# Attention with a depthwise convolution: the first image ends like the middle ones, the first q and k piece follows the projection, and constant products run at the start

## The chip, the core and the metric

The kernel runs on one core of a Trainium2 chip. A core has TensorE (PE in the profile, its weight loads PEld), VectorE (DVE), ScalarE (ACT), GpSimd (POOL) and SyncE (SP). Each engine works through its own instructions in order; data transfers are issued by SP, ACT or POOL instructions and run beside the engines. The metric is the time of one execution in microseconds (us) on the device; less is better.

## The reference

The input x holds 16 images of 384 channels and 32 x 32 points. Two layers follow each other, each with a residual:

```python
x = x + attention(_gn(x), w_qkv, w_proj, b_proj)     # 8 heads of 48 channels, softmax over 1024 points
x = x + depthwise_conv7x7(_gn(x), w_sym)             # w_sym: mean of the four rotations of weight
```

`_gn` normalises 32 groups of 12 channels to mean 0 and variance 1 over all points of a group. All is float32.

## The kernel before

**Tiling.** Channels lie on the 128 partitions, three tiles (k or o = 0, 1, 2) to an image. The heads are taken in pairs: unit u = 4b + p is pair p of image b. A unit has two halves of 512 query points, and each half eight steps, one for every 128 key points. So an image has 64 steps, in eight groups of eight (r = 0, 8, ..., 56).

**A step.** `s_step` (L466) makes the scores of both heads in one PSUM buffer, and ScalarE takes the exponential out of it (L480). `av_step` (L482) multiplies with the values. The values carry a column of ones, so the row sums of the softmax come out of the same products. After eight steps `take` (L499) copies a half out of PSUM. The tag "s" has three PSUM buffers, shared by scores, q and k, values and projections, in turn.

**The order.** The program order is written out by hand: the scheduler of the framework is off (`manual_schedule`). The main loop (L1155) writes, for each group: eight `s_step`; in the group r = 0 of an image also its value products (`v_step`, L442, 15.7 us on PE); a slot for other work; eight `av_step`; another slot. A planner counts two clocks in us, `clock` for PE and `vclock` for VectorE, with fixed costs (L808). `after(wait, cost, f)` puts off a piece of VectorE's work, `catch_up` (L872) writes what is due and fills up with convolution taps, `applies` with `act_slot` (L967) holds ScalarE's pieces with a due time and a cost, and `other` (L1111) starts a projection if one is due, or else the next piece of q and k of the next image (`chunks`; one piece is two `qk_step`, L414, 12 products and two ScalarE copies, L428). The last piece, "rest", is six copies between partitions on SP (L437).

**A middle image's end.** `finish` (L1022) sends the row sums out through DRAM (SP, L506 and L507), `invert` takes the reciprocal on 16 columns and spreads it back (L513 to L519), `divide` multiplies (L524), and the fourth unit's rows are copied to the other three (six SP transfers, L529), so that the projection needs three packed weights `w_packed`. This takes place while the next image's first scores and values are made. Then `project` (L913) writes three `proj_step` (L534: 6 products, an ACT output with the row sum, a POOL transfer that adds x, L556); behind the second it writes the normalisation of the image after next on ScalarE (`x_apply`, L338, three tiles). Then come the statistics of the result x1: `x1_means` on VectorE (L943), `x1_squares` on ScalarE (L270), a trip through DRAM on POOL (`gather_x1`, L276 and L278), `aggregate` (L282), `groups_x1` on ScalarE (L288 to L290), a second trip on POOL (`spread`, L259 and L263), and `x1_chains` (L974): ScalarE normalises three tiles (L338), and VectorE starts the 49 taps of each (L607).

**The ends of images 0 and 15** (`FAST`, L139) are different: the sums are spread by a product with a mask (`divide_at_once`, L568), the reciprocal is taken on 512 columns (L570), and the projection is split into parts with four weights, one for each unit (`proj_part`, L579; weights `w4` in `wp` and `w3`). For image 0, `fast_finish` and `fast_end` lie between its last value products and image 1's first ones. `fast_end` makes the statistics with one-column products on PE (`groups_on_pe`, L307) and normalises on POOL, ACT and DVE. At the start, image 0's own x is normalised with `groups_on_pe` too.

**Once only.** In image 0, VectorE takes the statistics of the images 2 to 15 as they stream in. At the end of group r = 0 of image 1, `conv_prepare` (L632) is written: on POOL a memset, two transfers to DRAM, 16 transfers back (L648, which wait for the first), eight transfers of zeros (L658, L659) and four small operations on `eye` (L663, L665). They prepare the part of the last two images' convolution that PE does. After it SP loads `wp` anew with `w_packed` (L1206).

Of the kernel before, what the change touches and what calls it, by code (L numbers as in the profile page):

```python
# [16 lines left out]
P = 128  # L17
# [27 lines left out]
def kernel(  # L45
# [64 lines left out]
    def run(general):  # L110
        tag = "g" if general else "f"
        with ExitStack() as stack:
# [20 lines left out]
            def psum(name):  # L133
                return ps_s.tile([P, 2, HALF], F32, tag="s", name=name)
# [1 line left out]
            xns, x1s, qks, os_, accs, es, xn1s = {}, {}, {}, {}, {}, {}, {}  # L136
            xds, shs, pss, mats, psums = {}, {}, {}, {}, {}
            PE_K = [NK - 1, NK - 2]
            FAST = (0, B - 1)  # L139

            PE_TILES = [(b, k) for b in (B - 2, B - 1) for k in PE_K]
            SHARED = None if general else (B - 2, PE_K[1])
# [27 lines left out]
            w4 = w_proj_4.rearrange("(t p) c -> p t c", p=P)  # L170
            w_packed = w_proj_t.rearrange("(k p) c -> p k c", p=P)
            late, pps = {}, {}
            if general:
                nc.sync.dma_start(wp, w_packed)
            else:
                nc.sync.dma_start(wp, w4[:, 0:NK])
                late["w3"] = npool.tile([P, N], F32, tag="xn1", name="w3_0")[:, 0:C]
                nc.sync.dma_start(late["w3"], w4[:, NK])
            bp = wpool.tile([P, NK], F32, name="bp")
            with nc.allow_non_contiguous_dma(reason="one small vector"):  # L180
                nc.sync.dma_start(bp, b_proj.rearrange("(k p) -> p k", p=P))
# [379 lines left out]

            def divide_at_once(u, h):
                half = os_[u][:, h * HALF : (h + 1) * HALF]
                ps = ps_o.tile([P, HALF], F32, tag="acc", name=f"ps_sum_{u}_{h}")
# [249 lines left out]
            def now():  # L817
                return vclock if catching else max(clock, vclock)

            def after(wait, cost, f):  # L820

                nonlocal count
                count += 1
                heapq.heappush(later, (now() + wait, count, cost, f))
# [88 lines left out]
            def project(b):  # L913
                nonlocal clock
                for o in range(NK):
                    proj_step(b, o)
                    clock += US_PROJ
                    if b in ON_VECTOR:
                        after(8.0, 1.3, lambda o=o: x1_part(b, o))

                    if o == 1 and pending:
                        pending.pop()()
                if b not in ON_VECTOR:
                    after(1.6, 0.2, lambda: x1_means(b))

            def x1_part(b, k):

# [12 lines left out]
            def x1_means(b):  # L940
                st = x1_stats[b] = Stats(f"x1_{b}")
                st.bs = x1_bs[:, b % 2]
                nc.vector.scalar_tensor_tensor(  # L943
                    st.bs[:, :, 1::3],
                    psums.pop(b).unsqueeze(2).to_broadcast([P, NK, 2]),
                    -1.0 / N,
                    x_mean[:, b, :].unsqueeze(2).to_broadcast([P, NK, 2]),
                    ALU.mult,
                    ALU.add,
                )  # L950
                applies.append((now() + 4.5, 4.2, lambda: x1_squares(b, st)))

            def x1_squares(b, st):
                for k in range(NK):
                    st.square(x1s[b, k], k)
                st.gather_x1()
                after(11.0, 0.6, lambda: x1_aggregate(b, st))
# [16 lines left out]
            def x1_chains(b, st):  # L974
                on_pe = [t for t in PE_TILES if t[0] == b]
                for k in range(NK - 1, -1, -1):
                    conv_begin(st, b, k, (nc.gpsimd, None, nc.vector)[k] if b in (0, B - 1) else None)
                    if (b, k) in on_pe:
                        conv_store(b, k)
                        pe_conv.extend(  # L980
                            (b, k, h, part)
                            for h in range((b, k) == SHARED, 2)
                            for part in range(2)
                        )
                after(
                    2.0 if b == B - 1 else 6.0,
                    0.0,
                    lambda: chains.extend(
                        (b, k) for k in range(NK) if (b, k) not in on_pe or (b, k) == SHARED
                    ),  # L990
                )
# [29 lines left out]

            def finish(u):  # L1022
                sums_out(u)
                if u % NP < NP - 1 or u // NP not in FAST:
                    waiting.add(u)
                    after(6.0 if u % NP == NP - 1 else 9.0, 0.3, lambda: finish2(u))

# [11 lines left out]
            def queue(b):  # L1039
                chunks.extend(("qk", b, i) for i in range(6))  # L1040
                chunks.append(("rest", b, 0))

            st = Stats("x_0")
            for k in range(NK):
                st.channels(xns[0][:, k, :], k)
# [2 lines left out]
            for k in range(NK):  # L1048
                engine = (nc.vector, None, nc.vector)[k]
                st.apply(xns[0][:, k, :], xns[0][:, k, :], k, engine)  # L1050
            conv_weights()
            ready[0] = 0.0
            queue(0)
            every = [(b, k) for b in range(2, B) for k in range(NK)]
# [100 lines left out]
            for b, n0, size in [  # L1155
                (b, b * PER_B + sum(SIZES[:g]), SIZES[g]) for b in range(B) for g in range(len(SIZES))
            ]:
                r = n0 - b * PER_B
                if n0 == NS - PER_B:
                    last_image = clock  # L1160
                if r == 0:
                    while chunks:
                        issue(chunks.popleft())
                    if b + 1 < B:
                        queue(b + 1)
                for n in range(n0, n0 + size):
                    s_step(n)
                clock += (size * US_STEP + US_TURN) / 2
                if r == 0 and b - 1 == FAST[0]:
                    fast_end(b - 1)  # L1170
                if r == 0:
                    for i in range(NT // 2):
                        issue(("v", b, i))
                ending = b in FAST and r + size == PER_B
                if ending:
                    catch_up(clock)
                    divide_at_once(NP * b + NP - 1, 0)
                    vclock += 4.2
                    for o in range(NK):
                        proj_part(b, o, (0, 1))  # L1180
                    clock += 2 * US_PROJ
                else:
                    if r and pending and b - 1 in FAST:
                        applies.append((clock, 3.7, pending.pop()))
                    catch_up(clock)
                    act_slot(4.5)
                    other(r + size, False)
                for n in range(n0, n0 + size):
                    av_step(n)
                    u, h, i = n // (2 * NT), n // NT % 2, n % NT  # L1190
                    if i == NT - 1:
                        take(u, h)
                clock += (size * US_STEP + US_TURN) / 2
                if n0 // (2 * NT) < (n0 + size) // (2 * NT):
                    finish((n0 + size) // (2 * NT) - 1)
                if ending:
                    catch_up(clock)
                    assert not invs and not waiting
                    fast_finish(b)
                else:  # L1200
                    other(r + size, True)
                if b == B - 4 and r == 32:
                    after(0.0, 2.0, check_early)
                if b == 1 and r == 0:
                    conv_prepare()
                    nc.sync.dma_start(wp, w_packed)  # L1206
                if b == B - 1:

                    if once("mat_0", r >= 16):
                        mat = flat2(xpool.tile([P, NK, N], F32, tag="x", name="mat_0"))  # L1210
                        conv_matrices(0, mat)
                        late["w3"] = mat[:, 2 * SH * KS * CH :][:, 0:C]
                    if once("w", r >= 32 and b - 1 in x1_stats):
                        nc.sync.dma_start(wp, w4[:, 0:NK])
                        nc.sync.dma_start(late["w3"], w4[:, NK])
                    if once("mat_1", r >= 24):
                        conv_matrices(1, flat2(qkpool.tile([P, 2, N], F32, tag="qk", name="mat_1")))
                    if once("ones", r >= 32):
                        t = opool.tile([P, N], F32, tag="o", name="masks_1")
                        nc.sync.dma_start(t, masks.rearrange("p b c -> p (b c)"))  # L1220
                        late["masks"] = t.rearrange("p (b c) -> p b c", c=P)
                if b in FAST:
                    if r >= 32 and (b, 0) not in x1s and all(c[0] > b - 2 for c in active):
                        for k in range(NK):
                            x1s[b, k] = rpool.tile([P, N], F32, tag="x1", name=f"x1_{b}_{k}")
                            nc.gpsimd.dma_start(
                                x1s[b, k], x[b, k * P : (k + 1) * P].rearrange("p h w -> p (h w)")
                            )
                if b == B - 1 and r in (32, 40, 48):
                    loads(1)  # L1230
# [63 lines left out]
```

## Time and profile before

| | |
|---|---|
| median of 3 runs | 2950.46 us (2949.72 to 2952.27) |
| the profiled execution's own time | 2951.93 us |
| its span, from first to last instruction | 2950.1 us |
| mean granted TensorE clock | 0.997 |
| period of a middle image on PE (its projection at 426.12, the next at 601.4) | 175.3 us |
| ACT exponentials L480 | 952.4 us in 1024, 1054 ns each |
| DVE taps L607 | 2352.8 us in 2181, 1154 ns each |
| q and k products L421 | 509.1 us, 1152 records |

A line of the page or of an answer gives a source line, an engine, an operation, the tiles it writes and reads with their shapes, a count, and a busy time. In brackets stands how long the engine sat idle before it, and what ended that. A timeline line begins with start and length in us from the span's start; instructions of the same kind are merged. Lines for waits have the waiting line, what it waited for, the sum in us, how often, and the longest. A row of windows has the stretch, its length, the busy time of PE, PEld, DVE, ACT and POOL with instruction counts, the granted clock (1.00 is full), and the share and rate of the transfers.

The start in short: x lands by 7.9 us, VectorE's statistics are done at 9.6, two rounds of averages with one-column products run on PE from 9.67 and 13.47 (3.15 us each), and the first q product starts at 19.00.

### The profile page before, as it was taken

To read this page: it belongs to the slowest core of one execution; us is meant where nothing else is said; L and a number is where in the kernel's file an instruction comes from. 1 tells how busy PE (TensorE), PEld (TensorE's weight loads), DVE (VectorE), ACT (ScalarE), POOL (GpSimd) and SP (SyncE) were. 2 spreads that over 40 slices of the span, in tenths; PEclk is the share of its full clock that TensorE was granted. 3 is DMA by queue.
4 is the path that set the end of the run, shared out by engine and by line. 5 is a ranking of instruction groups with operands and counts; after the bars stand their busy time and mean duration, and the time that the engine had idled before them with its cause. 6 is when DMAs were issued, how large, how long until landed. Compare 5 with 4: busy or idle time off the path is not lost.

```text
span 2950.1 us, 30344 instructions
## 1 busy us (share of the span) xinstructions
PE 2921.9 (99%) x11590; PEld 1189.3 (40%) x11590; DVE 2576.3 (87%) x2582; ACT 1421.5 (48%) x1694; POOL 198.9 (7%) x303
## 2 busy tenths in 40 slices
PE   8999999999999999999999999999999999999998
PEld 4334343343434334343443434334343433434334
DVE  4417964989989898998989989898998999999997
ACT  2533445545454544545555454554545454454610
POOL 2213000010000001000010000001000000100000
PEclk9999999999999999999999999999999999999999
DMA  6511030131212212030121212113121221202324
GB/s 232 198 19 49 15 87 17 32 75 24 63 37 53 51 26 63 30 74 30 39 72 26 56 37 62 41 28 76 26 64 37 49 55 26 60 34 53 103 64 116
DMA packets 72460, 169.70 MB, mean 58 GB/s; under 512 B 30080, under 2 KB 32496, under 8 KB 70768
## 3 DMA queue, kind: packets, MB, share of 16 engines
q0 software_dynamic: 29328, 96.07, 12.0%
q1 hardware_dynamic: 41216, 67.98, 9.6%
q10 hardware_dynamic: 1760, 3.61, 0.5%
q8 instruction: 93, 1.52, 0.2%
q14 instruction: 63, 0.52, 0.1%
HBM read 120.18 MB, written 29.34 MB: 51 GB/s over the span
## 4 chain that ended last, share of the span: by engine, by line
PE 86%; DVE 6%; issue 6%; DMA 1%; POOL 0%; ACT 0%; SPq 0%; POOLq 0%; DVEq 0%; ACTq 0%
PE ps_s L472 27%; PE acc L488 27%; PE ps_qk L421 16%; PE ps_v L447 8%; PE ps_proj L541 6%; DVE x L607 5%; PE ps_conv L712 1%; PE ps_proj L579 1%; DVE sum L607 0%; DMA x<-in_x 0%; PE ps_st_x L307 0%; DMA inv<-inv 0%; DMA sh<-xd 0%; DVE bs_x L239 0%; DVE o L524 0%
## 5 line engine op out<-in xcount | busy, mean ns | idle before, releaser
L607 DVE SCALAR_TENSOR_TENSOR x<-xn,wsym,x 128x899 f32<-128x899 f32 (+11 forms) x2181 | 2352.8, 1154 | 140.7 <-ACT xn L338 139.7
L480 ACT ACTIVATE e<-ps_s 128x1024 f32<-128x1024 f32 x1024 | 952.4, 1054 | 60.1 <-PE ps_s L472 56.2
L472 PE MATMUL ps_s<-qk 48*128 48x512 f32 x4096 | 914.3, 596 | 0.3 <-ACT e L480 0.3
L488 PE MATMUL acc<-e,v 128*64 128x512 f32 x4096 | 907.1, 595 | 0.0
L472 PEld LDWEIGHTS ps_s<-qk 48*128 48x128 f32 x4096 | 376.4, 185 | 533.7 <-ACT e L480 258.5
L488 PEld LDWEIGHTS acc<-e,v 128*64 128x64 f32 x4096 | 282.8, 137 | 608.2 <-issue 603.6
L421 PE MATMUL ps_qk<-x,wqk 128*128 128x512 f32 x1152 | 509.1, 599 | 2.4 <-DVE x L334 2.4
L499 ACT COPY o<-acc 128x512 f32<-128x512 f32 x128 | 75.2, 587 | 681.8 <-PE acc L488 681.8
L421 PEld LDWEIGHTS ps_qk<-x,wqk 128*128 128x128 f32 x1152 | 216.0, 191 | 294.0 <-issue 288.1
L447 PE MATMUL ps_v<-wv,x 128*128 128x384 f32 x768 | 253.9, 491 | 0.0
L428 ACT COPY qk<-ps_qk 128x1024 f32<-128x1024 f32 x96 | 96.9, 1009 | 285.0 <-PE ps_qk L421 285.0
L541 PE MATMUL ps_proj<-o,wp 128*128 128x512 f32 x504 | 218.6, 592 | 0.0
L447 PEld LDWEIGHTS ps_v<-wv,x 128*128 128x128 f32 x768 | 145.6, 191 | 109.9 <-ACT e L480 11.4
L456 ACT COPY v<-ps_v 128x384 f32<-128x384 f32 x128 | 55.1, 483 | 186.3 <-PE ps_v L447 186.3
L541 PEld LDWEIGHTS ps_proj<-o,wp 128*128 128x128 f32 x504 | 95.8, 190 | 117.6 <-issue 112.6
L155 POOL DMA_DIRECT2D x<-in_x x42 | 22.4, 542 | 1631.5 <-PE ps_v L447 1485.9
L549 ACT ACTIVATE x<-ps_proj,bp 128x1024 f32<-128x1024 f32 x42 | 46.8, 1113 | 126.4 <-PE ps_proj L541 126.4
L524 DVE TENSOR_TENSOR o<-o,inv 128x1024 f32<-128x1024 f32 x62 | 75.7, 1220 | 25.3 <-DMA inv<-inv 21.2
L338 ACT ACTIVATE xn<-x,sc_x 128x1024 f32<-128x1024 f32 x44 | 51.6, 1235 | 82.6 <-DMA sc_x<-gr_x 55.0
L712 PE MATMUL ps_conv<-sh,mat 128*32 128x496 f32 (+3 forms) x784 | 83.2, 580 | 1.7 <-DMA sh<-xd 1.7
L361 DVE BATCH_NORM_STATS2 bs_all<-xs 128x6 f32<-128x512 f32 x84 | 51.9, 680 | 11.2 <-DMA xs<-in_x 11.2
L556 POOL DMA_DIRECT2D x<-in_x x42 | 36.6, 871 | 311.4 <-ACT x L549 302.0
(113 smaller groups left out, 559.5 us busy)
## 6 DMA issues: line engine op xcount, KB each, us to landing
x<-in_x POOLq DMA_DIRECT2D x90, 512.0 KB, 5.5
inv<-inv SPq DMA_DIRECT2D x124, 256.0 KB
out<-x POOLq DMA_DIRECT2D x48, 512.0 KB, 3.8
xs<-in_x POOLq DMA_DIRECT2D x42, 512.0 KB, 6.3
qk<-qk SPq DMA_DIRECT2D x96, 128.0 KB
sh<-xd SPq DMA_DIRECT2D x34, 160.0 KB
o<-o SPq DMA_DIRECT2D x84, 64.0 KB
sh<-xd ACTq DMA_DIRECT2D x22, 160.0 KB
```

Source lines behind the costliest of these rows:

```text
L421: nc.tensor.matmul(ps[:, h, :], lhsT=wqk[:, k, s, t, :], rhs=xns[b][:, k, h * HALF : (h + 1) * HALF], start=(k == 0), stop=(k == NK - 1),)
L428: nc.scalar.copy(halves(qks[u][:, s, :]), ps)
L447: nc.tensor.matmul(ps[:, j, 0:C], lhsT=xns[b][:, k, t * P : (t + 1) * P], rhs=wv[:, k, :], start=(k == 0), stop=(k == NK - 1),)
L456: nc.scalar.copy(dst.rearrange("p (h d) -> p h d", d=D + 1)[:, :, 0:D], ps[:, j, 0:C].rearrange("p (h d) -> p h d", d=D),)
L472: nc.tensor.matmul(ps[:, j, :], lhsT=qks[u][r, 1, i * P : (i + 1) * P], rhs=qks[u][r, 0, h * HALF : (h + 1) * HALF], start=True, stop=True,)
L480: nc.scalar.activation(es[n], ps, AF.Exp, scale=SCALE)
L488: nc.tensor.matmul(accs[u, h][64 * j : 64 * j + 64, :], lhsT=v_of(u, i, j), rhs=e[:, j, :], start=(i == 0), stop=(i == NT - 1),)
L499: nc.scalar.copy(os_[u][:, h * HALF : (h + 1) * HALF], accs.pop((u, h)))
L524: nc.vector.tensor_tensor(os_[u], os_[u], invs.pop(u), ALU.mult)
L541: nc.tensor.matmul(ps[:, h, :], lhsT=wp[:, t, o * P : (o + 1) * P], rhs=os_[NP * b + t][:, h * HALF : (h + 1) * HALF], start=(t == 0), sto ...
L607: nc.vector.scalar_tensor_tensor(acc, xn1s[b, k].rearrange("p (h w) -> p h w", w=W)[:, iy, ix], wsym[:, k, dy + PAD, dx + PAD : dx + PAD + 1],
L712: nc.tensor.matmul(pss[b, k][CH * i : CH * (i + 1), h, :].rearrange("p (y x) -> p y x", x=W)[:, :, ox], lhsT=mats[k][:, i, d0 * KS + dx + ...
```

## The change

- `FAST` is gone. Image 0 ends by `finish`, `invert`, `divide`, `project` and `x1_means` like the images 1 to 13; only image 15 keeps the separate end. Image 0's x1 is normalised on ScalarE alone. The means of image 0's x are kept (`means_of`) for this.
- `wp` is loaded with `w_packed` at the start; the loads of `w4` and `w3` there, and the reload in image 1, are gone.
- `project` writes the first piece of the next q and k right behind its third part, with `catch_up` and `act_slot(9.0)` between its two steps, if that image's x is normalised by then in the program order. Before, it was written in the slot after the value steps.
- `x1_squares` is due 1.0 us after `x1_means` in the planner's clock, for 4.5.
- Eight products of 128 x 384 on the tile `v`, which holds ones from a POOL memset (2.20 to 5.04 us), are written ahead of the first statistics. Nothing reads their output.

```diff
-            FAST = (0, B - 1)
...
-            if general:
-                nc.sync.dma_start(wp, w_packed)
-            else:
-                nc.sync.dma_start(wp, w4[:, 0:NK])
-                late["w3"] = npool.tile([P, N], F32, tag="xn1", name="w3_0")[:, 0:C]
-                nc.sync.dma_start(late["w3"], w4[:, NK])
+            nc.sync.dma_start(wp, w_packed)
...
@@ project
                 if b not in ON_VECTOR:
                     after(1.6, 0.2, lambda: x1_means(b))
+                if chunks and b + 2 in ready:
+
+                    issue(chunks.popleft())
+                    catch_up(clock)
+                    act_slot(9.0)
+                    issue(chunks.popleft())
...
@@ x1_means
-                applies.append((now() + 4.5, 4.2, lambda: x1_squares(b, st)))
+                applies.append((now() + 1.0, 4.2, lambda: x1_squares(b, st)))
...
@@ x1_chains
-                    conv_begin(st, b, k, (nc.gpsimd, None, nc.vector)[k] if b in (0, B - 1) else None)
+                    conv_begin(st, b, k, (nc.gpsimd, None, nc.vector)[k] if b == B - 1 else None)
...
@@ finish
-                if u % NP < NP - 1 or u // NP not in FAST:
+                if u < U - 1:
...
+            warm = psum("warm")
+            for n in range(8):
+                nc.tensor.matmul(
+                    warm[:, n % 2, 0:C], lhsT=v[:, n, 0:P], rhs=v[:, n, 0:C], start=True, stop=True
+                )
             st = Stats("x_0")
...
             conv_weights()
+            means_of(st.bs, x_mean[:, 0, :])
...
@@ main loop
-                if r == 0 and b - 1 == FAST[0]:
-                    fast_end(b - 1)
...
-                ending = b in FAST and r + size == PER_B
+                ending = b == B - 1 and r + size == PER_B
...
-                    if r and pending and b - 1 in FAST:
-                        applies.append((clock, 3.7, pending.pop()))
...
                 if b == 1 and r == 0:
                     conv_prepare()
-                    nc.sync.dma_start(wp, w_packed)
...
-                if b in FAST:
+                if b == B - 1:
```

## The prediction

> **What bounds the kernel now.** I read the page first, then TensorE's waits, then the timeline of the two places where an image ends.
>
> ```profile
> PE 2921.9 (99%) x11590; PEld 1189.3 (40%) x11590; DVE 2576.3 (87%) x2582; ACT 1421.5 (48%) x1694; POOL 198.9 (7%) x303
> ```
>
> TensorE (PE) is busy in all but 28 us of the span: about 10 before its first product, some 12 after its last, the rest in its waits:
>
> ```profile
> PE ps_st_x L307 <- DVE mn_x L316: 9.7, 1, 9.7
> PE ps_qk L421 <- DVE x L334: 2.4, 1, 2.4
> PE ps_st_x L307 <- DVE d_x L322: 1.9, 3, 0.6
> ```
>
> So only fewer or faster products, or less of these waits, can shorten the kernel. Busy is not the same as fast, so I compare the end of image 0 with the end of image 1. The PE timeline, image 0 to 1 (start, length, line, records; each float32 product has two records):
>
> ```profile
> 205.61 1.12 PE L568 MATMUL ps_sum<-o,masks 128*128 128x512 f32 x2
> ...
> 237.86 5.42 PE L472 MATMUL ps_s<-qk 48*128 48x512 f32 x24 [0.33 <-ACT e L480]
> 243.21 1.72 PE L307 MATMUL ps_st_x<-mn_x,masks 128*128 128x1 f32 x14
> 245.57 3.05 PE L307 MATMUL ps_st_x<-d_x,masks 128*128 128x1 f32 x14 [0.64 <-DVE d_x L322]
> 248.48 17.73 PE L447 MATMUL ps_v<-wv,x 128*128 128x384 f32 x48
> 266.15 7.09 PE L488 MATMUL acc<-e,v 128*64 128x512 f32 x32
> ```
>
> From the last scores of image 0 (205.61) to the first value products of image 1 (266.15) are 60.54 us. The same stretch from image 1 to 2 runs from 396.45 to 441.66, 45.21 us. Between ends lie the clock rows (columns: PE, PEld, DVE, ACT, POOL busy, granted clock):
>
> ```profile
> 242.32:245.73 3.41, 2.77 (x22) 1.93 (x18) 0.48 (x3) 2.38 (x3) 0.00 (x0) 1.00 0.00 0
> 245.73:249.14 3.41, 3.41 (x15) 3.23 (x16) 0.16 (x1) 0.00 (x0) 0.17 (x1) 0.50 0.03 7
> ```
>
> The one-column products of L307 did not hold the clock: it fell 2.5 us after the dense products had stopped, and the v products after them paid for it.
>
> **First image ends like the middle ones.** Removed: image 0's projection with four packed weights (48 records at 0.43 us, 20.6) for three (36, 15.5): 5.2. Two L568 products: 1.7. The two averages with the wait between them, 243.21 to 248.48: 5.3. The v products at half clock, 17.7 instead of 15.75: 2.0. The 0.33 wait and smaller joints make up the rest of the difference of the two stretches: **60.54 - 45.21 = 15.3 us off PE's path**. VectorE loses two L570 (3.36 each), three residuals and six statistics; it isn't the bound there. SyncE loses the reload of wp and the load of w3, and gets image 0's row sums, inverse and nine copies more. Image 1's six copies of L437 (3.7 us) go ahead of the inverse in that queue, but image 1's own end has 7.3 us from its last copy (418.8) to the projection (426.12), which hides them; uncovered, they cost 3.7 at most. ScalarE gets three squares and all three normalisations (3.5 us each set) into pauses like those of later images.
>
> **What this moves behind another queue.** Call P the end of image 0's projection on PE. In image 1 the same moment was 441.66 and the rest of its statistics went so (the timeline of all engines):
>
> ```profile
> 453.07 0.80 POOL L276 DMA_DIRECT2D ch_x<-x_bs  x1 [8.96 <-ACT sq_x L270]
> 455.85 0.53 POOL L278 DMA_DIRECT2D gs_x<-ch_x  x1 [1.98 <-DMA ch_x<-x_bs]
> 471.53 0.60 POOL L259 DMA_DIRECT2D gr_x<-af_x  x1 [15.15 <-ACT af_x L290]
> ...
> 478.14 3.51 ACT L338 ACTIVATE xn<-x,sc_x 128x1024 f32<-128x1024 f32 x3 [4.18 <-DMA sc_x<-gr_x]
> 481.55 0.99 ACT L428 COPY qk<-ps_qk 128x1024 f32<-128x1024 f32 x1
> 483.76 7.14 PE L472 MATMUL ps_s<-qk 48*128 48x512 f32 x32
> ```
>
> Already here ScalarE stands 4.18 us before L338, with two copies of q and k and eight exponentials behind it; PE just escapes, since the second score step needs the PSUM buffer freed by the first copy at 482.5 only at 484.6: 2.1 us to spare. In image 0 the statistics now share POOL with conv_prepare, written at the end of image 1's first group. By the planner's clock (c at the projection's end) the squares with L276 and L278 are written at c+5.3, conv_prepare after c+17.6, and L259 at c+24.7, in the next group. So L259 stands behind all of it:
>
> ```profile
> 268.47 0.22 POOL L636 MEMSET zero<- 128x128 f32 x1
> 268.62 0.78 POOL L639 DMA_DIRECT2D w_d<-wsym  x1
> ...
> 274.64 0.57 POOL L648 DMA_DIRECT2D wsh<-w_d  x1 [4.47 <-DMA w_d<-wsym]
> ...
> 287.88 4.89 POOL L663 COPY eye<-ident 128x32 f32<-128x32 f32 x1
> 292.85 3.26 POOL L665 TENSOR_TENSOR eye<-eye,ident 128x32 f32<-128x32 f32 x3
> ```
>
> Before, this took 268.47 to 296.11, 27.6 us, and nobody waited. Now: the squares end at P+10.0, L278 at P+13.6, and conv_prepare begins. Its first wait (6.2 from its start) lay behind three 512 KB loads; the small store L276 was followed after 2.78, so with the second store 0.92 later I take 3.7, and 25.2 for the whole. L259 goes at P+38.8 instead of P+29.9; L338 6.6 later at P+45.4, the first copy done at P+49.8 (3.4 + 1.0). PE wants that buffer at P+43.0, so it idles 6.8. Then its score steps are paced by exponentials of 1.05 us, some at half clock, since such a gap is longer than the 2.5 us after which it fell: I make the group end 8.4 after the copy, P+58.2 (7.1 at full clock), against P+49.1. **Cost: 9.1 us.** Bounds: with the old wait for w_d, 11.5; with a short L663 5.2, and 3.9 without the slow clock; nothing only if L259 were not behind conv_prepare, and a gain is excluded, since POOL only gets more to do.
>
> Here a rule speaks for the lower bound. The row is L663's 4.89 us beside 0.99 to 1.13 for each of the three L665 on the same 32 columns. The Trainium skill (GPSIMD Engine Reference, section Specifications) has POOL sharing its SBUF ports with VectorE, with contention when VectorE reads two SBUF inputs. L607 does so, and it ran through the whole of L663; in the new place it is still waiting. By the rule L663 shrinks to some 1 us and the total is 2940; by the row, whose three neighbours ran beside the same L607 at 1 us, L663 has a cost of its own and the total is 2944. I go by the row.
>
> **First piece of q and k behind the projection.** 12 products and two copies are moved ahead of 8 value steps, with no DMA; PE's total is unchanged. What it gives up is cover: the normalised x is done 0.45 us before the projection's end (L338's three end at 441.2), and the first product needs only the first third, done 2.4 before. It is alike in the 13 images I looked at. The squares' earlier due time (1.0 for 4.5) puts them between the two copies, P+6.5 to P+10.0, where ScalarE was idle; the third needs x1's third load (issued at P+1.6, 5.6 to land, 7.9 at most) by P+8.8. A late one delays the second copy (P+10.7), which nobody needs before P+17.5. Later steps stay in their groups, so the chains begin as before: 0.
>
> **Products on constants.** Eight products of 384 columns (16 records) from 5.05 (v's memset ends at 5.04). Cold v records of this trace took 0.64, warm ones 0.33. The clock rose 5.0 us after the dense start at 19.00 and 4.0 after that at 248.48; with that, the 16 end near 12.8, and the averages that began at 9.67 wait 3.1. They run at 1.72 instead of 3.15 each: 2.9 back. The Trainium skill (TensorE: Matmul & The Clock Gate, section Why this matters for your kernels) says to warm up with at least 4 us of matmuls; by that alone the first q product would also run fast (its first copy came 7.85 after the start against 5.45 warm), a gain of 2.4, 2.2 net. The row 245.73 says that the averages do not hold the clock, and from 12.8 to the q products are 6.7 us of little but them. So **0**, between -2 and +2.5.
>
> **Sum.** 2951.93 (profiled execution; span 2950.10, 1.83 around it) - 15.3 + 9.1 + 0 = 2945.7; the median shown is 1.5 below it: **2944**. The tail (PE dense to 2937.9, VectorE's last tap 9 us earlier) keeps its order and follows.
>
> **Rivals.** *No wait in image 1*: L259 is not held, or its delay fits ScalarE's pause: 2950.5 - 15.3 = 2935. For it: little on POOL is needed soon; against it: 2.1 us of slack against 8.9 of delay. *Nothing is left*: conv_prepare at its old 27.6 and a start at +2.5 give 2949. *Slower*: the piece behind the projection finds x not normalised. Place: L338 at the projection's second part; price: its lateness beyond 0.45 us, in 14 images; it decides from 0.44 us each (14 x 0.44 = 6.2), and 1 us beyond that gives 2958. For it: ScalarE is in order and the loads land as little as 2.5 us before L338. Against it: L338 never waited for a load after the first image.
>
> **Numbers.** Forecast (2940 to 2948) 0.66; no or short wait (2933 to 2940) 0.24; nothing left (2948 to 2952) 0.07; slower 0.03. A change under 0.2% (5.9 us) can't be told from none. The forecast lies just beyond that line (2944.6): 0.42 of its 0.66 counted as faster with the 0.24, the rest with the 0.07 as same. Range 2935 to 2949.
>
> **What would show it.** Right: PE runs from image 0's last scores to image 1's first value products, less the moved piece, in about 45 us; one PE wait of some 7 us on ScalarE some 43 us after P, ended by L338, which waited for sc_x; L259 right after L665. Wrong: no such wait; the clock at 1.00 when q begins; a wait of PE on L338 in every image.

## The result, and the profile after

| | before | after |
|---|---|---|
| median of 6 runs | 2951.36 us | 2933.74 us (2931.85 to 2935.46) |
| ratio | | 0.994, interval 0.9927 to 0.9953 |
| profiled execution, its span | 2951.93, 2950.1 us | 2935.46, 2933.7 us |
| 13 image periods on PE (first value product of image 2 to that of image 15) | 2278.90 us | 2276.63 us |

The kernel became 17.6 us faster; 6 to 7 had been forecast, and the range ended 1.3 us above the result. In the new source the lines from about L170 on stand 6 or 7 higher up (L338 is L332, L421 is L415, L259 is L253, L663 is L656). PE's row of the page, and its two longest waits (after; the others are 1.3 and 0.5 us in all):

```profile
PE 2911.8 (99%) x11562; PEld 1174.2 (40%) x11562; DVE 2559.9 (87%) x2565; ACT 1433.9 (49%) x1713; POOL 192.6 (7%) x305
```

```profile
PE warm L1045 <- POOL v L181: 5.1, 1, 5.1
PE ps_qk L415 <- DVE x L328: 2.4, 1, 2.4
```

What is absent from the list is the wait of the scores for ScalarE, some 7 us, on which the forecast rested. PE at the end of image 0 (after):

```profile
206.30 7.09 PE L482 MATMUL acc<-e,v 128*64 128x512 f32 x32
...
251.42 10.46 PE L415 MATMUL ps_qk<-x,wqk 128*128 128x512 f32 x24
...
293.41 7.43 PE L466 MATMUL ps_s<-qk 48*128 48x512 f32 x32
```

From the last scores of image 0 (206.30) to the end of its projection (251.42) are 45.1 us where 60.5 were, 15.4 less. The score group at 293.41, behind which the wait was expected, takes 7.43 for 7.14. What POOL did meanwhile (after):

```profile
268.37 8.68 POOL L641 DMA_DIRECT2D wsh<-w_d  x16 [1.25 <-DMA w_d<-wsym]
...
281.32 0.22 POOL L656 COPY eye<-ident 128x32 f32<-128x32 f32 x1
281.63 0.90 POOL L658 TENSOR_TENSOR eye<-eye,ident 128x32 f32<-128x32 f32 x3
282.83 0.64 POOL L253 DMA_DIRECT2D gr_x<-af_x  x1 [0.30 <-issue]
```

The statistics' second trip (L253, before L259) does stand right behind conv_prepare, as forecast. But the copy took 0.22 us and not 4.89, the three sums 0.90 and not 3.26. VectorE is what differs. In the old place its taps ran beside all four, with one short reciprocal between (before, then after):

```profile
251.90 40.79 DVE L607 SCALAR_TENSOR_TENSOR x<-xn,wsym,x 128x1024 f32<-128x1024 f32 x38 [1.02 <-POOL xn L334]
```

```profile
293.31 3.68 DVE L600 SCALAR_TENSOR_TENSOR x<-xn,wsym,x 128x1024 f32<-128x1024 f32 x3 [26.03 <-ACT xn L332]
```

In the new one it stood idle for 26 us, until image 0's taps could start at 293.31. So ScalarE's wait grew only from 4.18 to 6.15 (its timeline, after):

```profile
289.76 3.51 ACT L332 ACTIVATE xn<-x,sc_x 128x1024 f32<-128x1024 f32 x3 [6.15 <-DMA sc_x<-gr_x]
293.18 1.90 ACT L422 COPY qk<-ps_qk 128x1024 f32<-128x1024 f32 x2
```

The 16.4 us between the two profiled spans: the start lost 0.7 (first scores at 53.18 for 52.49), the end of image 0 gave 15.4, the score group of image 1 cost 0.3, the moved piece of image 1 gave 0.2, the 13 later periods 2.3 together, and the tail lost 0.5.

### The profile page after: what moved, and what is told of

Read it like the earlier page. It is cut to its first block, busy times and chain, and to the rows that moved or that the text cites. A ratio compares the mean times of both kernels' runs of the same rounds, so it can differ in the third digit from the quotient of the medians.

```text
span 2933.7 us, 30301 instructions
## 1 busy us (share of the span) xinstructions
PE 2911.8 (99%) x11562; PEld 1174.2 (40%) x11562; DVE 2559.9 (87%) x2565; ACT 1433.9 (49%) x1713; POOL 192.6 (7%) x305
## 4 chain that ended last, share of the span: by engine, by line
PE 86%; DVE 7%; issue 5%; DMA 1%; POOL 0%; ACT 0%; POOLq 0%; SPq 0%; DVEq 0%; ACTq 0%
PE ps_s L466 27%; PE acc L482 27%; PE ps_qk L415 16%; PE ps_v L441 8%; PE ps_proj L535 7%; DVE x L600 6%; DVE sum L600 1%; PE warm L1045 0%; DVE o L518 0%; DMA inv<-inv 0%; DMA out<-x 0%; DMA gr_x<-af_x 0%; DVE bs_x L233 0%; ACT sq_x L264 0%; PE ps_st_x L301 0%
## 5 line engine op out<-in xcount | busy, mean ns | idle before, releaser
L415 PE MATMUL ps_qk<-x,wqk 128*128 128x512 f32 x1152 | 507.7, 597 | 2.4 <-DVE x L328 2.4
L415 PEld LDWEIGHTS ps_qk<-x,wqk 128*128 128x128 f32 x1152 | 217.2, 191 | 289.4 <-issue 286.9
L535 PE MATMUL ps_proj<-o,wp 128*128 128x512 f32 x540 | 234.2, 592 | 0.0
L535 PEld LDWEIGHTS ps_proj<-o,wp 128*128 128x128 f32 x540 | 102.6, 190 | 126.0 <-issue 119.8
L154 POOL DMA_DIRECT2D x<-in_x x42 | 22.3, 539 | 1644.1 <-PE ps_v L441 1607.9
L332 ACT ACTIVATE xn<-x,sc_x 128x1024 f32<-128x1024 f32 x46 | 53.9, 1235 | 89.9 <-DMA sc_x<-gr_x 65.7
L705 PE MATMUL ps_conv<-sh,mat 128*32 128x480 f32 (+3 forms) x784 | 83.0, 580 | 0.1
L507 DVE RECIPROCAL rec<-sums 128x16 f32<-128x16 f32 x63 | 15.5, 247 | 72.5 <-DMA sums<-sum 72.5
```

What stands on the lines that cost most here:

```text
L415: nc.tensor.matmul(ps[:, h, :], lhsT=wqk[:, k, s, t, :], rhs=xns[b][:, k, h * HALF : (h + 1) * HALF], start=(k == 0), stop=(k == NK - 1),)
L535: nc.tensor.matmul(ps[:, h, :], lhsT=wp[:, t, o * P : (o + 1) * P], rhs=os_[NP * b + t][:, h * HALF : (h + 1) * HALF], start=(t == 0), sto ...
L705: nc.tensor.matmul(pss[b, k][CH * i : CH * (i + 1), h, :].rearrange("p (y x) -> p y x", x=W)[:, :, ox], lhsT=mats[k][:, i, d0 * KS + dx + ...
```

## The experiments

The ratio of a run is to runs of the kernel before on the same chip. The cuts of code are shortened, and the comments in them belong to this text. The changed kernel once more:

> The changed kernel itself, as the standard for the three beside it on the same chip: 2933.7 us if nothing drifts.

Measured: 2932.42 us (2931.79 to 2935.31), ratio 0.9938 (0.9924 to 0.9951). What follows is compared with the two medians, 2932.4 and 2933.7.

**VectorE beside the operations on eye.** Four runs fill VectorE with scratch work while POOL does conv_prepare; the kernel's result does not use it (`wqk_flat` stands for the weights `wqk` seen as one row). The first two:

```diff
                 if b == 1 and r == 0:
                     conv_prepare()
+                    junk = npool.tile([P, N], F32, tag="xn1", name="junk")     # dve_two
+                    nc.vector.memset(junk, 0.0)
+                    for _ in range(25):
+                        nc.vector.scalar_tensor_tensor(junk, wqk_flat[:, 0:N], wsym[:, 0, 0, 0:1], junk, ALU.mult, ALU.add)
...
+                    junk = small.tile([P, 6], F32, tag="junk", name="junk")    # dve_one
+                    for _ in range(43):
+                        nc.vector.bn_stats(junk, wqk_flat[:, 0:HALF])
```

> The changed kernel with 25 extra VectorE instructions of two SBUF inputs (scalar_tensor_tensor on 128 x 1024, some 1.2 us each, on a scratch tile) written behind conv_prepare, so that VectorE reads two inputs while POOL does the five small operations on eye. Theory (the copy and the three sums on eye were slow before the change because VectorE held the shared ports, and fast after it because VectorE stood idle): the four take 8 us again instead of 1.1, the normalisation of image 0's x1 starts 7 us later, PE waits 6 to 7 us once in image 1, and the time is 2942 (8.5 more), which is the loss that the prediction had put there. Rival A (the long copy was a cost of first use): the four stay at 1.1 and the time at 2934. Rival B (ScalarE's pause has room for it): the four take 8 us and the time stays at 2934.

Measured: 2943.60 us (2940.37 to 2945.11), ratio 0.9968 (0.9957 to 0.9979). The three sums took 3.92 (3.26 before the change), the copy only 0.27. PE lost 3.6 in image 1's score group, not 8.5. The time came out near the expected one for another reason: the scratch work ran 33 us, to 301.3, past the moment when image 0's taps could begin, and VectorE was late with a division: PE waited three times, 4.9 us in all, for the copies of o before image 1's projection. A time that agrees shows nothing when the waits don't.

> The same with 43 bn_stats on 128 x 512, which have one SBUF input and write six numbers, for the same 29 us of VectorE. If two inputs are what takes the ports: the four operations on eye stay at 1.1 us and PE does not wait. If a busy VectorE of any kind is enough: 8 us and a wait of 6 to 7 us.

Measured: one run of 2941.45 us, so its time decides nothing. Copy 0.22, sums 0.91, and no wait for ScalarE in image 1. VectorE was busy for 31 us here too, so a busy VectorE alone is not what stretches POOL. What bn_stats lacks is the second input and also the full-width output; no run separates the two. The same lateness came before the projection (4.5 us).

The next two end before the taps can start, so they leave VectorE's later work alone:

```diff
+                    for _ in range(16):                      # dve_tap: one tile, in the form of a tap
+                        nc.vector.scalar_tensor_tensor(jv[:, 1:H, 1:W], wv3[:, 0 : H - 1, 0 : W - 1], wsym[:, 0, 0, 0:1], jv[:, 1:H, 1:W], ALU.mult, ALU.add)
...
+                    for i in range(18):                      # dve_three: the same on three tiles in turn
+                        jv = junks[i % 3].rearrange("p (h w) -> p h w", w=W)
```

> The changed kernel with 16 VectorE instructions of the form of a convolution tap (31 x 31 points out of 32 x 32, two SBUF inputs, 1.2 us each) on a scratch tile, written behind conv_prepare and over before image 0's chains can start. In the run with 25 contiguous two-input instructions the three sums on eye took 3.9 us again but the copy stayed at 0.3. Theory (what made the copy long is the form of the taps beside it): the copy takes 4 to 5 us and the sums 3, L253 is issued 7 us later, PE waits 6 to 7 us in image 1, and the time is 2942 to 2943, with no wait of a projection. Rival (the copy's length has another cause): only the sums grow, PE loses 3.6 us in image 1, and the time is 2936.

Measured: 2938.87 us (2938.08 to 2939.56), ratio 0.9953 (0.9937 to 0.9968). Sums 3.73, copy 0.64: the form of the taps is not it. The score group took 12.8 from its start to its end, 5.4 more than after; the rival had said 3.6. PE's wait was 2.0, nearly as in `dve_two` (1.9), but the granted clock stood at half for 6.8 us behind it, and for 3.4 in `dve_two`.

> As the run with 16 taps on a scratch tile, but 18 of them in turn on three scratch tiles, so that no tap waits for the one before it, as the real taps of three chains do not. With one tile they took 1.25 us each, with the real chains 1.15. Theory (the copy on eye gets the ports only in the gap between dependent taps; without the gap it waits as it did before the change): copy 4 to 5 us, sums 3, L253 issued some 7 us later than in the changed kernel, PE waits 6 to 7 us in image 1, and the time is 2942 to 2943. Rival (the copy was long for another reason): copy under 1, sums 3 to 4, PE loses 4 to 5 us, and the time is 2938.

Measured: 2943.14 us (2942.46 to 2944.57), ratio 0.9973 (0.9961 to 0.9984). POOL's timeline and then VectorE's, of this run:

```profile
280.00 9.33 POOL L656 COPY eye<-ident 128x32 f32<-128x32 f32 x1
289.42 0.90 POOL L658 TENSOR_TENSOR eye<-eye,ident 128x32 f32<-128x32 f32 x3
290.62 0.64 POOL L253 DMA_DIRECT2D gr_x<-af_x  x1 [0.30 <-issue]
```

```profile
268.97 20.29 DVE L1214 SCALAR_TENSOR_TENSOR junk<-wqk,wsym,junk 128x961 f32<-128x961 f32 x18
```

The copy ended at 289.33, when the unbroken stream of two-input instructions had ended at 289.26; the sums behind it were short. So the copy itself is short: it waits for a break in VectorE's stream, and how long depends on when the next one comes. In the kernel before, the taps of three chains gave way to a reciprocal (L513) at 292.61, and the copy, begun at 287.88, ended at 292.77. Where each instruction needs the one before it (one scratch tile), the times suggest breaks between them: 1.25 us apiece for 1.13 on three tiles. What makes a break stays open. Beside the same unbroken taps of the kernel before, each of the three sums got through in about the time of one tap (1.0 to 1.1), and the MEMSET on POOL, which reads nothing, took 0.22 there as it does beside an idle VectorE.

This run also tests the chain behind the copy. The statistics' trip came at 40.7 us after the projection's end (forecast for the changed kernel: 38.8), PE waited 8.4 and its score group lost 10.4 (forecast: 9.1), and the time rose by 9.4 to 10.7.

**The chain of the wait, without VectorE.**

```diff
                     nc.gpsimd.dma_start(xds[bk][:, (PAD + H) * W :], zero)
+                    nc.gpsimd.dma_start(xds[bk][:, 0 : PAD * W], zero[:, 0 : PAD * W])
+                    nc.gpsimd.dma_start(xds[bk][:, (PAD + H) * W :], zero)
```

> The changed kernel with conv_prepare's eight small transfers of zeros issued twice: 8 x 0.54 = 4.3 us more on POOL ahead of the statistics' second trip, VectorE as idle as before. Theory (the wait chain of the prediction: POOL, ScalarE's normalisation, the copies of q and k, PE's buffers, with no slack left in the changed kernel, whose score group already takes 0.3 longer): PE waits 4.3 us, in part at half clock afterwards, and the time is 2938.5 to 2940. Rival (slack on ScalarE): 2934.

Measured: 2945.17 us (2943.13 to 2947.97), ratio 0.9978 (0.997 to 0.9986), more than expected, since the doubled transfers write the same place and waited for each other: L253 came at P+41.8 (P is the projection's end, as in the prediction), 10.4 later than in the changed kernel and not 4.3. PE's timeline of this run:

```profile
292.02 1.13 PE L466 MATMUL ps_s<-qk 48*128 48x512 f32 x4
302.65 9.54 PE L466 MATMUL ps_s<-qk 48*128 48x512 f32 x28 [9.51 <-ACT qk L422]
```

This is the very picture that the forecast drew: the first score step runs, the second waits for the copy of q and k, and the rest needs 9.5 us after it (forecast: 8.4). With nothing else touched, POOL's lateness reaches PE nearly whole: of 10.4 us, 9.5 are PE's wait. With the half clock behind the wait the score group lost 12.7, and the time rose by 11.4 to 12.8.

```diff
-                if b == 1 and r == 0:
+                if b == 1 and r == 16:
                     conv_prepare()
```

> The changed kernel with conv_prepare written two groups later, at the end of group r = 16 of image 1, behind both trips of image 0's statistics. Theory: the score group of image 1 takes 7.14 instead of 7.43, ScalarE's wait falls from 6.15 to about 4.2, and the time is 0.3 below the changed kernel, not to be told from it. Rival (conv_prepare still holds something up): a difference of 2 us or more.

Measured: 2933.76 us (2932.26 to 2934.32), ratio 0.9938 (0.9921 to 0.9954). The score group took 7.14, ScalarE's wait 4.34. The copy, now beside real taps, took 4.31 and the sums 3.2, and nobody waited for them. The copy ended at 305.20, 0.07 after a division of VectorE (303.91 to 305.13); the change from the taps to that division, at 303.91, had not let it through. So conv_prepare costs the changed kernel 0.3 us, below what the times can tell.

**The three parts of the change.**

```diff
-            warm = psum("warm")                                   # no_warm
-            for n in range(8): ...
...
-                if chunks and b + 2 in ready: ...                 # piece_back
-                applies.append((now() + 1.0, 4.2, lambda: x1_squares(b, st)))
+                applies.append((now() + 4.5, 4.2, lambda: x1_squares(b, st)))
```

> The changed kernel without the eight constant products. Theory (the constant products only delay the first averages, and the clock has fallen again before the q products): the first q product starts at 19.0 instead of 19.6, the clock at that moment is not full in either, and the time is 2933.1, within 1.5 of the changed kernel either way. Rival (they hold the clock for the q products, worth about 2): 2936.

Measured: 2933.37 us (2931.96 to 2935.09), ratio 0.9939 (0.9926 to 0.9953): no difference. First q product at 18.94, first scores at 51.55.

> The changed kernel with the first q and k piece in its old slot behind the value steps, and the squares due after 4.5 as before. Theory (each change of PE between full and partial tiles of the array costs 0.1 us, and the piece behind the projection saves two of them in each of 14 images): the period of an image on PE goes from 175.1 back to 175.3, and the time to 2936.4 (2.7 more). Rival (the 2.3 us that the middle images gained come from the squares, the loads or the clock): the period stays at 175.1 and the time at 2933.7.

Measured: 2937.06 us (2935.85 to 2938.80), ratio 0.9951 (0.9937 to 0.9964), 3.3 to 4.6 more than after. The period is back at 175.3 (the 13 periods: 2279.30). Of the rest, its profile has a wait of 2.9 in the tail for the transfers of sh, which the changed kernel hasn't.

`end_only` is both together: only the end of image 0 is changed.

> Only the end of image 0 changed: no constant products, the q and k piece in its old slot, the squares due after 4.5. Theory (the end gives 15.4 less some tenths in image 1, the piece 2.7, the constant products 0 on average): 2951.9 - 15 = 2937. Rival (the piece behind the projection is needed for the gain of the end): 2940 or more.

Measured: 2935.80 us (2935.27 to 2937.33), ratio 0.9942 (0.9928 to 0.9956). So the end of image 0 alone brings nearly all, some 16 to 17 us; the piece and the constant products bring 2 to 3 together.

`due_back` leaves the piece behind the projection and gives only the squares their old due time (4.5 for 1.0):

> The changed kernel with the squares due 4.5 after the means again, the piece staying behind the projection. By the planner's clock they are then not due between the two steps of the piece and go one group later, 14 us. Theory (VectorE has only some 10 us to spare in an image): the chains of every image start 14 us later, VectorE falls behind, divisions come late and PE waits before projections and in the tail: 2940 to 2960. Rival (the squares' time does not matter): 2933.

Measured: 2955.44 us (2955.12 to 2956.45), ratio 1.0011 (1.0003 to 1.002). One constant of the planner takes away the whole gain and some more, though PE's products up to the tail ran as in the changed kernel (the 13 periods: 2276.61): the waits before projections that had been expected did not come. In this run the squares of image 0 began at 275.8, in the changed one at 257.7; in a middle image they began at 626.1 for 608.2, with PE at the same place in both. So they come 18 us later, not 14. The first taps behind them come 25 to 27 us later (318.0 for 293.3 in image 0, 668.3 for 641.7 in that middle image). VectorE's last sum, in `due_back` and then after:

```profile
2940.82 1.23 DVE L860 TENSOR_TENSOR x<-x,sum 128x1024 f32<-128x1024 f32 x1
```

```profile
2912.97 1.23 DVE L860 TENSOR_TENSOR x<-x,sum 128x1024 f32<-128x1024 f32 x1
```

PE's last product ended at 2919.4 in the one and at 2921.1 in the other. VectorE's last sum ends 7 us ahead of it in the changed kernel (2914.2), and in `due_back` 23 us behind it (2942.1): there VectorE is the one that ends last. That sum comes 28 us later than in the changed kernel, about as much as the first taps of these two images.

**The start.**

```diff
-            st.groups_on_pe(late["masks"])
+            st.groups_on_pe(late["masks"], fill)     # at its second call: two products of 128 x 352 on v, the eight are gone
```

> The changed kernel with the constant products not before the first statistics but in PE's pause between the second average and the first q product: two products of 352 columns, which need 2.3 us at half clock where PE waits 2.4. Theory (the clock rises after a full stretch of dense products, wherever it begins, and a pause filled costs nothing): the clock is full about 2.4 us sooner after the start of the q products, and the time is 1 to 2 us below the kernel without constant products: 2932. Rival (these products do not count, or the averages ahead of them undo it): as without constant products, 2933.1.

Measured: 2931.77 us (2930.97 to 2933.04), ratio 0.9934 (0.992 to 0.9947). First scores at 50.85.

> A version put together from what the runs pointed to: the changed kernel with the constant products in PE's pause before the first q product, and conv_prepare two groups later. Theory: 0.3 us from conv_prepare and about 1 from the start: 2931.5, some 1 to 2 us below the changed kernel. Rival (neither is more than noise): 2932.5 to 2933.7.

Measured: 2932.51 us (2930.95 to 2933.48), ratio 0.9931 (0.9918 to 0.9945). First scores at 50.64. By time, none of these versions can be told from the changed kernel. The moment of the first scores says more, since every run's profile gives it: with the eight constant products it was 51.43 to 53.18, 52.3 on average, in ten profiles; without them 51.55, 52.21 and 52.49; with the pause filled 50.85 and 50.64. The spread is wide: 53.18 and 51.43 are two profiles of the same changed kernel. But both filled ones lie below all the others, and the step between q's weight loads halves from 0.85 to 0.43 (full clock) 2.7 and 1.0 us after the first q product, for 3.3 to 5.2 in the others. So filling the pause gains about 1.4 us at the start, by two profiles, and the eight products ahead of the statistics show no gain.

## Why the prediction was wrong, point by point

**The end of image 0** was sized right: 15.3 forecast, 15.4 measured.

**The wait in image 1** is the step that failed, in one term: "by the row, whose three neighbours ran beside the same L607 at 1 us, L663 has a cost of its own". The copy and the three sums had been carried over with 8.2 us; they took 1.1. The rest of that sum held: L278's end at P+13.9 (forecast 13.6), L648's start at P+17.0 (17.3). With 7 us less, L253 went at P+31.4 and not at P+38.8, the first copy of q and k was ready when PE came for it, and the 9.1 shrank to 0.3. The Trainium skill's line on the shared ports (GPSIMD Engine Reference, section Specifications) had been right and was overruled: `dve_two`, `dve_tap` and `dve_three` brought the long times back, `dve_one`, with one input and little output, did not. The neighbours on which I overruled it were no witnesses: at 1 us they were slowed about fourfold themselves (0.25 to 0.30 each beside an idle VectorE or after its stream). And the bound that I drew from the rule, 2940, cut only the copy; cutting all four would have left a delay of 1.9 us, inside PE's slack of 2.1, and a total near the 2935 of the first rival.

That the mechanism behind the step was right is shown by `dve_three` and `pool_late`: when POOL is as late as I had it, or later, PE loses 10.4 and 12.7 us. One premise of the forecast was loose: the clock does not fall a fixed 2.5 us after the products stop. In `dve_two` it fell with a wait of only 1.9. It was a correct chain with a wrong duration at its head, taken from a place where the operation had stood in other company.

**"PE's total is unchanged"** for the moved piece was the second error, and the reason why even the right rival was 1.3 too high. Each period is 0.2 us shorter; `piece_back` undoes it, and so does `end_only` (2279.31 for the 13 periods), but `due_back` does not (2276.61): the moved piece makes it, not the due time of the squares and not the end of image 0. Where it comes from is seen in the weight loads of the first q product, before and then after:

```profile
448.67 0.30 PEld L421 LDWEIGHTS ps_qk<-x,wqk 128*128 128x128 f32 x2 [0.81 <-issue]
```

```profile
251.42 0.19 PEld L415 LDWEIGHTS ps_qk<-x,wqk 128*128 128x128 f32 x1 [0.24 <-issue]
```

Behind value products, which use half the columns of the array, the next weight load came only after a gap of 0.81 us; behind the projection, which uses the whole array like q and k, the loads follow in their usual step of 0.24. Projection and piece took 15.45 and 10.4 us from start to start, for 15.54 and 10.5. Two such joints of somewhat under 0.1 us each in 14 images make the 2.5 us of the 13 periods and image 1. That the joint is due to the array's shape is argued from these two places; no run varied the shape by itself.

**No cost at the piece** was right: no wait of PE on L332 in any image. **"The chains begin as before: 0"** was right as well, but what hung on it was not seen: without the new due time they begin 25 to 27 us later, and the time is 22 us longer.

**The constant products**: 0, between -2 and +2.5, held. In the profiled run they delayed the q products by 0.6 (in `after_again` not at all), and the clock rows show that they could not help (columns: PE, PEld, DVE, ACT, POOL busy, granted clock, transfers; up to 17.10 the clock was 1.00):

```profile
17.10:20.50 3.40, 1.02 (x3) 0.55 (x3) 2.11 (x5) 1.24 (x1) 2.91 (x5) 0.60 0.24 40
20.50:23.90 3.40, 3.40 (x5) 1.35 (x4) 2.46 (x8) 0.00 (x0) 1.45 (x3) 0.50 0.87 342
23.90:27.30 3.40, 3.40 (x8) 1.48 (x7) 2.58 (x5) 0.00 (x0) 1.10 (x3) 0.89 1.00 378
```

If the clock in these rows is either 1.00 or 0.50, it went down at about 17.8, 4.4 us after the constant products had ended (13.4), with only averages and a pause in between, and came back at about 24.6, 5.0 us after the first q product (19.61). In the ten profiles with these products the fall lies 3.0 to 4.4 us after their end and the return always 6.8 us after the fall, 3.0 to 5.0 into the q products. In none did the clock hold until q began. In `after_again`, the same program, q began 0.7 us sooner, the clock fell at 15.0 and was back at 21.9, and the first scores came 1.75 us sooner.

**The chances**: the rival without a wait, at 0.24, was the one that came.

## What to carry to other kernels

When an operation moves, its duration has to be asked for anew: see which engine ran beside it in the old place and in the new one, and hold a long row against the shortest row of its kind in the trace, not against its neighbours in the same company. Here products of one array shape side by side saved 2.5 us, and filling a pause of PE that existed anyway did more than work put ahead of it. A due time in a hand-written planner is part of the change: moved code that is no longer due in its slot can cost more than the change brings.

## What the runs showed of the hardware

- A GpSimd copy of 128 x 32 took 0.22 us beside an idle VectorE and beside bn_stats, 0.27 and 0.64 beside dependent two-input instructions, 4.89 and 4.31 beside real taps, and 9.33 beside independent ones. In the last three it ended 0.07 to 0.08 us after the end of a VectorE instruction, with several of them back to back before. The sums took 0.25 to 0.30 apiece alone and 1.0 to 1.3 beside two-input work. A MEMSET (0.22) and POOL's issue of transfers (0.54 each) did not change.
- PE gained a little under 0.1 us at each joint between products of the full and of half the array that the change removed (2.27 us in 13 images with two joints each); that the array's shape is the reason is argued.
- One-column products did not keep the clock up: with only such products and pauses, it fell 3.0 to 4.4 us after the dense ones had stopped at the start (ten profiles), and 2.5 us after at image 0's end (before).
- The stretches at half clock lasted 3.4 us (`dve_two`), 6.8 (the start of ten profiles, image 0's end before, `dve_tap`), 10.2 (`dve_three`) and 13.7 (`pool_late`), each a whole multiple of 3.41.
